# Seven products for eight in one dense layer, and an eigenvalue iteration moved ahead of it

## The chip, the cores and the metric

The kernel runs on one core of a Trainium2 chip. The metric is the device time of one execution in microseconds (us); lower is better. Three runs of the kernel before gave 2445.72, 2446.64 and 2447.99 us, a median of 2446.64.

The engines are named as in the profile: PE is the matrix engine TensorE (PEld its weight loads), DVE is VectorE, ACT is ScalarE, POOL is GpSimd, and SP is the queue that issues most DMA transfers. The built program is one list of instructions for each engine, and the trace shows every engine taking its own list in order; semaphores connect the lists.

## The reference, cut to what matters

Four layers follow each other on x of shape [128, 64, 256] (128 graphs of 64 nodes with 256 features), each with a residual connection and a layer norm. Everything is in fp32. The change lies in layer 0, and in the eigenvalue that layer 1 needs:

```python
# layer 0
A_norm = A + eye;  A_hat = A_norm * dinv[:, None] * dinv[None, :]
agg = einsum('nm,bmd->bnd', A_hat, features)
h   = relu(_batchnorm(agg @ W1.T + b1, g1, be1))      # 512 wide
out = _batchnorm(h @ W2.T + b2, g2, be2)              # 256 wide
x   = _layernorm(x + out)
# layer 1 begins with
lam_max = eigvalsh(L)[-1] + 1e-08
L_norm  = 2.0 * L / lam_max - eye
xp = einsum('mn,bnf->bmf', L_norm, x);  h = xp @ Wc + bc;  ...
```

Both batch norms take mean and variance over all 8192 rows. So no relu can start before the first dense product is complete for every row, and nothing after the second product can start before that one is complete for every row.

## The kernel before, in words

**Tiling.** The 8192 rows are cut into 16 blocks of 512 rows (`NBLK`, `TB`). A block's rows are spread over 128 partitions of two graphs each. Feature-major tiles hold 128 features on the partitions and the 512 rows along the free dimension; a helper `fm` views a buffer of 1024 columns as two such chunks. The two buffers of a block, `Xs[i]` and `H[i]`, hold the four chunks of the 512-wide hidden layer: chunks 0 and 1 in `Xs[i]`, 2 and 3 in `H[i]`.

**Layer 0.** `first_block(i)` loads a block (L525), multiplies it with `A_hat` on PE (`aggregate`, L320, eight matmuls of 128 columns), copies it out of PSUM on DVE (L535), multiplies it with W1 in two halves of four matmuls of 512 columns (`mm_fm`, L344), adds the bias on ACT (L547) and takes batch statistics on DVE (L551). When all 16 are done, `bn_coeffs` (L506 to L513) turns the statistics into a scale and a shift; the inverse root is one POOL instruction (L509). `second_block(i)` then applies relu with that scale and shift on ACT to the four chunks (L559), multiplies by W2 with eight matmuls of 512 columns (L564: two output chunks times four input chunks), adds the bias on ACT (L573), and takes statistics on DVE (L577). A second `bn_coeffs` follows, and `end_block` normalises (L636), transposes back on PE (L338), adds the residual (L644) and does the layer norm (L270, L272, L306, L309, L312).

**The eigenvalue.** `eig()` squares the 128 x 128 matrix M 26 times on PE (`EIG_STEPS`; L466). After each square, DVE takes the diagonal (L469, L471), PE sums it over the partitions with a matrix of ones (L474), and DVE takes the reciprocal of that trace (L477) and scales the square with it (L479). At the end L484 to L497 form the Rayleigh quotient and the matrix `LnT` that layer 1 multiplies with. `eig` has a PSUM buffer of its own (`e_ps`) out of four.

**Order.** The order of the work is made by a planner written in the kernel, `flow`. Tasks are generators that yield steps (engine, expected time, PSUM and SBUF buffers wanted); the planner always takes the step that can start soonest by its own estimate, with a margin of 2.0 us for PE steps, and of equal ones the task with the higher rank. In layer 0 there is one stream of at most six tasks at a time, and `eig` is the second task in it. The framework below may still move single instructions where their operands allow. The names that the text uses besides: `W2T` is W2 as loaded (L403), `Wc` to `W2` of layer 1 are loaded at L607 (W2 into the second half of `WB`), `end_block`'s input at L633, and at the head of the layers that follow L853 (wL), L370 (Wg, av), L860 (Wx), L379 (biases) and L896 (WT) are loads, L882 and L884 small products of the adjacency matrix with their copies L887 and L888, and L903 a product with one column (av).

Of the kernel before, what the change touches and what calls it, by code (L numbers as in the profile page):

```python
# [10 lines left out]
AF = mybir.ActivationFunctionType  # L11
# [4 lines left out]
P = 128  # L16
B, N, D = 128, 64, 256
NBLK = 16
TB = 512
# [14 lines left out]
def kernel(ctx: ExitStack, tc: tile.TileContext, a: dict, out: bass.AP):  # L34
# [15 lines left out]
    def fm(s):  # L50

        return s.rearrange("p (c k) -> p c k", c=2)
# [45 lines left out]
    class Stream:  # L98
# [3 lines left out]

        def __init__(self, width, prio, tasks):
            self.width, self.prio, self.tasks, self.n = width, prio, tasks, 0

    done = {}

# [3 lines left out]
    def ready(*keys):  # L113

        if all(k in done for k in keys):
            return max([0.0] + [done[k] for k in keys])
        return None

    def step(e, us, ps=0, sl=0, waits=True, at=None, tbl=None):

        return (e, us, ps, sl, waits, at, tbl)

    def flow(streams, margin):

        free = dict.fromkeys("TVSGQ", 0.0)
        table, running, now, seq = None, [], 0.0, 0
        while True:
            for s in streams:
                while s.tasks and s.n < s.width:
                    cond, body, peak = s.tasks[0]  # L140
                    t = 0.0 if cond is None else cond()
                    if t is None:
                        break
                    s.tasks.pop(0)
                    Clock.end, Clock.task = max(t, now), None
                    g = body()
                    if g is not None:
                        s.n += 1
                        seq += 1
                        running.append([(s.prio, seq), g, next(g), Clock.end, peak, 0, s])  # L150
                        running.sort(key=lambda r: r[0])
            if not running:
                assert not any(s.tasks for s in streams), "a task can't begin"
                return
            best, when, least = None, 0.0, 0.0
            lack = sorted((r[4] - r[5], r[5], r[0]) for r in running)

            def safe(r, sl):
                left = len(mem.free) - sl
                for short, held, rank in lack:  # L160
                    if r is not None and rank == r[0]:
                        short, held = short - sl, held + sl
                    if short > left:
                        return False
                    left += held
                return True

            mem.withdraw(lambda: safe(None, 1))
            for r in running:
                e, us, ps, sl, _, at, tbl = r[2]  # L170
                at = at() if callable(at) else at
                if r[2][5] is not None and at is None:
                    continue
                t = r[3] if at is None else at
                soon = max(t + margin.get(e, 0.0), free[e])
                t = max(t, free[e])
                if (ps <= 0 or len(PS.free) >= ps) and (sl <= 0 or (len(mem.free) >= sl and safe(r, sl))):
                    if ps > 0:
                        t = max(t, PS.free[0][0])
                        soon = max(soon, PS.free[0][0])  # L180
                    if sl > 0:
                        t = max(t, heapq.nsmallest(sl, mem.free)[-1][0])
# [27 lines left out]
    def ctile(shape, name, pool=cp):  # L210
        return pool.tile(shape, F32, tag=name, name=name)
# [152 lines left out]
    def by_chunk(ap):  # L364
        return ap.rearrange("(k p) m -> p k m", p=P)
# [19 lines left out]
    with c0:  # L385
# [7 lines left out]
        cols = {k: ctile([P, 4 if j < 3 else 2], f"l0{k}", wp) for j, k in enumerate(("b1", "g1", "be1", "b2", "g2", "be2"))}  # L393
        nc.scalar.dma_start(cols["b1"], a["L0_gnn_b1"])
        W2T = ctile([P, 4, D], "W2T", wp)

        def later_loads():
            for k in cols:
                if k != "b1":
                    yield step("Q", 1.0)  # L400
                    nc.sync.dma_start(cols[k], a[f"L0_gnn_{k}"])
            yield step("Q", 6.0)
            nc.sync.dma_start(W2T, by_chunk(a["L0_gnn_W2"]))  # L403
            yield step("V", 1.2)
# [36 lines left out]

        def eig():
            yield step("V", 1.2)
            V.tensor_scalar(Sy, Sy, 0.5, None, ALU.mult)
# [13 lines left out]
            V.tensor_scalar(sh, sh, 1e-30, None, ALU.add)  # L460
            M = etile("eM")
            V.scalar_tensor_tensor(M, ident, sh, Sy, ALU.mult, ALU.add)
            for _ in range(EIG_STEPS):
                yield step("T", 0.5)
                pm = pse(P)
                T.matmul(pm, M, M, start=True, stop=True)  # L466
                yield step("V", 0.6)
                t_ = etile("etmp")
                V.tensor_tensor(t_, pm, ident, ALU.mult)  # L469
                d_ = etile("ed", 2)  # L470
                V.reduce_sum(d_[:, 0:1], t_, axis=AX.X)  # L471
                yield step("T", 0.4)
                p_ = pse(2)
                T.matmul(p_[:, 0:1], ones, d_[:, 0:1], start=True, stop=True)  # L474
# [79 lines left out]
        def second_block(i):  # L554
            sc1, sh1 = bn["bn1"]
            src = [(fm(Xs[i]) if f < 2 else H[i])[:, f % 2, :] for f in range(4)]
            yield step("S", 2.8)
            for f in range(4):
                S.activation(src[f], src[f], AF.Relu, scale=sc1[:, f : f + 1], bias=sh1[:, f : f + 1])  # L559
            yield step("T", 6.9, ps=1)  # L560
            ps = PS.take()
            for c in range(2):
                for f in range(4):
                    T.matmul(  # L564
                        fm(PS[ps])[:, c, :],
                        W2T[:, f, c * P : (c + 1) * P],
                        src[f],
                        start=(f == 0),
                        stop=(f == 3),
                    )  # L570
            yield step("S", 1.3, ps=-1)
            for c in range(2):
                S.activation(H[i][:, c, :], fm(PS[ps])[:, c, :], AF.Identity, bias=cols["b2"][:, c : c + 1])  # L573
            PS.give(ps)
            yield step("V", 1.25)
            for c in range(2):
                V.bn_stats(st2[:, c, i, :], H[i][:, c, :])  # L577
            mark("l0b", i)

        blocks = range(NBLK)  # L580
        tasks = [(None, lambda i=i: first_block(i), 2) for i in blocks]
        tasks[1:1] = [(None, eig, 0)]
        tasks[4:4] = [(None, later_loads, 0)]
        tasks.append(
            (
                lambda: ready(*[("l0a", i) for i in blocks]),
# [1 line left out]
                0,  # L588
            )
        )  # L590
        tasks += [(lambda: ready(("bn1",)), lambda i=i: second_block(i), 0) for i in blocks]
        tasks.append(
            (
                lambda: ready(*[("l0b", i) for i in blocks]),
# [1027 lines left out]
```

## Time and profile before

| | |
|---|---|
| median of three runs | 2446.64 us |
| the profiled execution | 2449.05 us |
| its span, first to last instruction | 2447.3 us |
| PE busy in the span | 2362.6 us (97%) |
| DVE, ACT, POOL busy | 1208.8, 1152.1, 565.7 us |
| mean granted PE clock | 0.984 |
| first product's last W1 matmul starts a last time at | 155.2 us |
| second product L564, first start to last start | 161.7 to 277.0 us |
| first product of layer 1 (L320 with LnT) | 296.3 us |

Times within the kernel are microseconds from the start of the span of this one execution. An engine's busy time is the sum of its instructions; matmuls overlap in a pipeline and their ends are modelled, so the rate of a series of matmuls is read from the distance of their starts, not from the mean duration of one. In lists of groups, "x" is the number of instructions, then come busy time and mean duration in ns, and after the next bar how long the engine sat idle just before them and what it waited for.

### The profile page before, as it was taken

The page shows a single profiled execution, that of the slowest core. Times are in us where ns is not written, and L with a number is a line of the kernel's source. Part 1 is how long each engine was busy: PE and PEld are TensorE (multiplying, and loading weights), DVE is VectorE, ACT ScalarE, POOL GpSimd, SP SyncE. Part 2 cuts the span into 40 slices and gives each one's busy share as a digit, 9 for nine tenths or more (in the row PEclk, how much of TensorE's full clock was granted, in tenths as well). Part 3 has the DMA queues.
Part 4 walks back from the last instruction along what each step waited for, and adds up shares of the span by engine and source line. Part 5 has one row for each costly group of instructions (what it writes and reads, how often), then busy time and mean ns, then how long its engine had stood idle before and what let it go on. Part 6 is the DMA issues. An engine that isn't in the chain of part 4 may idle for free.

```text
span 2447.3 us, 33911 instructions
## 1 busy us (share of the span) xinstructions
PE 2362.6 (97%) x13700; PEld 1807.8 (74%) x13700; DVE 1208.8 (49%) x2868; ACT 1152.1 (47%) x2086; POOL 565.7 (23%) x426
## 2 busy tenths in 40 slices
PE   8999889989999999999999999999999999999986
PEld 5544566766775767666667888999999888888864
DVE  4542378564665455464442433354444554543465
ACT  2255454533444544444444444444435555653574
POOL 0000034231422233232322222222222222221111
PEclk9999899999999999999999999999999999999998
DMA  5110111100000000000010000000001001000201
GB/s 171 45 59 0 31 36 35 35 9 10 1 18 7 12 1 18 10 27 9 27 50 2 18 1 1 14 5 1 1 1 35 1 18 35 18 9 18 65 31 52
DMA packets 40973, 57.47 MB, mean 23 GB/s; under 512 B 4592, under 2 KB 33904, under 8 KB 40816
## 3 DMA queue, kind: packets, MB, share of 16 engines
q1 hardware_dynamic: 39712, 54.22, 6.8%
q8 instruction: 107, 1.75, 0.3%
q10 hardware_dynamic: 1104, 1.08, 0.1%
q14 instruction: 50, 0.41, 0.1%
HBM read 38.52 MB, written 16.78 MB: 23 GB/s over the span
## 4 chain that ended last, share of the span: by engine, by line
PE 73%; DVE 6%; ACT 4%; POOL 2%; issue 1%; POOLq 0%; ACTq 0%; DVEq 0%
PE ps L1022 24%; PE ps L950 13%; PE ps L344 10%; PE ps L356 5%; PE ps L833 4%; PE ps L320 3%; PE ps L703 2%; PE ps L1397 2%; PE ps L1159 2%; PE ps L1161 2%; DVE ln_st L270 1%; PE ps L332 1%; PE ps L776 1%; PE ps L1450 1%; ACT x L312 1%
## 5 line engine op out<-in xcount | busy, mean ns | idle before, releaser
L1022 PE MATMUL ps<-x,x 128*128 128x256 f32 x832 | 203.2, 379 | 0.7 <-DVE x L1090 0.7
L1022 PEld LDWEIGHTS ps<-x,x 128*128 128x128 f32 x832 | 155.0, 190 | 19.9 <-issue 1.1
L312 ACT ACTIVATE x<-x,ln_nm,ln_rs 128x256 f32<-128x256 f32 x176 | 92.9, 592 | 112.8 <-DVE ln_nm L309 112.8
L1022 PE MATMUL ps<-t,x 128*128 128x256 f32 x576 | 137.7, 380 | 0.0
L1022 PEld LDWEIGHTS ps<-t,x 128*128 128x128 f32 x576 | 108.4, 190 | 14.5 <-issue 0.4
L344 PE MATMUL ps<-t,W1T 128*128 128x512 f32 x256 | 115.1, 593 | 0.0
L306 POOL TENSOR_TENSOR ln_rs<-ln_rs,neghalf 128x4 f32<-128x4 f32 (+1 forms) x72 | 69.4, 964 | 189.7 <-DVE ln_rs L272 167.9
L950 PE MATMUL ps<-t,wL 128*128 128x512 f32 x216 | 94.5, 594 | 1.8 <-ACT t L1248 1.8
L292 POOL TENSOR_TENSOR ln_rs<-ln_rs,neghalf 128x4 f32<-128x4 f32 x32 | 35.9, 1122 | 239.5 <-DVE ln_rs L272 239.0
L950 PE MATMUL ps<-h,x 128*128 128x256 f32 x384 | 86.8, 379 | 0.0
L270 DVE BATCH_NORM_STATS2 ln_st<-x 128x6 f32<-128x256 f32 x224 | 85.5, 403 | 0.4
L962 ACT ACTIVATE t<-ps,bih 128x512 f32<-128x512 f32 (+3 forms) x108 | 63.5, 640 | 44.5 <-PE ps L950 44.4
L344 PE MATMUL ps<-t,wA 128*128 128x512 f32 x176 | 81.5, 608 | 2.6 <-ACT t L679 2.6
L1022 PE MATMUL ps<-h,x 128*128 128x256 f32 x320 | 82.5, 380 | 0.0
L1081 DVE COPY t<-ps 128x256 f32<-128x256 f32 (+2 forms) x58 | 21.6, 373 | 120.5 <-PE ps L1022 120.2
L344 PEld LDWEIGHTS ps<-t,W1T 128*128 128x128 f32 x256 | 46.3, 190 | 46.4 <-issue 46.4
L950 PEld LDWEIGHTS ps<-h,x 128*128 128x128 f32 x384 | 72.8, 190 | 10.2 <-issue 0.5
L950 PE MATMUL ps<-h,wL 128*128 128x192 f32 (+2 forms) x432 | 79.8, 338 | 0.0
L950 PEld LDWEIGHTS ps<-t,wL 128*128 128x128 f32 x216 | 40.7, 190 | 50.8 <-issue 47.1
L1098 ACT ACTIVATE x<-x,bih 128x512 f32<-128x512 f32 (+2 forms) x65 | 42.2, 650 | 76.2 <-DVE x L1088 73.9
L962 ACT ACTIVATE x<-ps,bih 128x512 f32<-128x512 f32 (+3 forms) x94 | 54.8, 636 | 45.6 <-PE ps L950 45.6
L950 PEld LDWEIGHTS ps<-h,wL 128*128 128x128 f32 x432 | 65.6, 190 | 11.4 <-issue 10.5
(681 smaller groups left out, 5765.3 us busy)
## 6 DMA issues: line engine op xcount, KB each, us to landing
t<-in_x_dram SPq DMA_DIRECT2D x28, 512.0 KB, 4.0
xd<-x SPq DMA_DIRECT2D x16, 512.0 KB, 2.6
x<-xd SPq DMA_DIRECT2D x5, 512.0 KB, 3.3
out_dram<-x SPq DMA_DIRECT2D x5, 512.0 KB, 2.9
wL<-in_L_gnn_Wih_dram SPq DMA_DIRECT2D x2, 1024.0 KB, 5.1
x<-in_L_gnn_Whh_dram SPq DMA_DIRECT2D x2, 1024.0 KB, 4.8
h<-in_x_dram SPq DMA_DIRECT2D x3, 512.0 KB, 5.0
t<-xd SPq DMA_DIRECT2D x3, 512.0 KB, 3.7
```

The costliest lines, as they stand in the source:

```text
L270: V.bn_stats(st[:, t, :], y[:, t, :])
L306: G.tensor_tensor(rs, rs, neghalf[:, :n], ALU.pow)
L312: S.activation(y[:, t, :], y[:, t, :], AF.Identity, scale=rs[:, t : t + 1], bias=nm[:, t : t + 1])
L320: T.matmul(ps[:, c, t * P : (t + 1) * P], y[:, t, c * P : (c + 1) * P], mT, start=True, stop=True,)
L344: T.matmul(ps[:, c, :], w[:, k, (off + c) * P : (off + c + 1) * P], yT[:, k, :], start=(k == 0), stop=(k == nk - 1),)
L356: T.matmul(ps[:, t, :], yT[:, k, t * P : (t + 1) * P], w[:, k, :], start=(k == 0), stop=(k == nk - 1),)
L703: T.matmul(pv[r * N : (r + 1) * N, b, :, :], x1T[:, k, b * N : (b + 1) * N], Wv_par[:, k, r, :, :], start=(k == 0), stop=(k == 1),)
L833: T.matmul(tm(PS[ps])[:, t, :], fm(mem[gs[k // 2]])[:, k % 2, t * P : (t + 1) * P], W2[:, k, :], start=(k == 0), stop=(k == 3),)
L950: T.matmul(spread(fm(PS[ps])[:, j, :n], q), WL[p][0][:, k, m], x_of(0, q)[:, k], start=(k == 0), stop=(k == 1),)
L962: S.activation(of(sl)[:, j], fm(PS[ps])[:, j, :n], AF.Tanh if g == 2 else AF.Sigmoid, bias=bias(g, c))
L1022: T.matmul(dst, WS[p][name](k, g), y[:, k], start=first and k == 0, stop=k == 1, skip_group_check=not first)
L1159: T.matmul(shaped(dst), WL[p][0][:, k, m], x[:, k], start=(k == 0), stop=False)
```

## The change

Three parts, all in layer 0.

The second product keeps its form for block 0 only, where it is now issued chunk by chunk: the relu of a chunk, then the two matmuls that use it. For blocks 1 to 15 the product is written with seven half-size products in place of eight (Strassen's form). The matrix W2 is cut in 2 x 2 quarters (each of 256 inputs and 128 outputs), and the block in input halves x, h and row halves u, v. DVE forms T1, T2 and T3 from differences of these quarters, POOL forms T4, and each of the seven products is two matmuls of 256 columns (L621 of the changed kernel). Partial results are taken out of PSUM on the way: two copies on ACT, one copy and two additions on DVE; the bias is added in three ACT instructions instead of two. Four combinations of quarters of W2 are formed once on DVE, and lie in the part of `WB` into which layer 1's W2 is loaded later.

In the eigenvalue iteration the trace is taken and divided out at every third square only; after the other squares DVE just copies the result out of PSUM.

`eig` becomes a stream of its own with the highest rank, whose steps have no margin in the planner, so that it runs as early as it can; the other tasks are the second stream. Its PSUM buffer is given back when it ends, and not after layer 0.

```diff
+        def __init__(self, width, prio, tasks, urgent=False):
...
-                soon = max(t + margin.get(e, 0.0), free[e])
+                soon = max(t if r[6].urgent else t + margin.get(e, 0.0), free[e])
...
+        W2S = WB[:, 2:4, :].rearrange("p a (b k m) -> p (a b) k m", b=2, k=2)
+        W2S = [W2S[:, j] for j in range(4)]
...
             nc.sync.dma_start(W2T, by_chunk(a["L0_gnn_W2"]))
+            yield step("V", 1.7)
+            (a11, a21), (a12, a22) = ([W2T[:, k : k + 2, c * P : (c + 1) * P] for c in range(2)] for k in (0, 2))
+            V.tensor_tensor(W2S[0], a21, a22, ALU.add)
+            V.tensor_tensor(W2S[1], W2S[0], a11, ALU.subtract)
+            V.tensor_tensor(W2S[2], a11, a21, ALU.subtract)
+            V.tensor_tensor(W2S[3], a12, W2S[1], ALU.subtract)
...
-            for _ in range(EIG_STEPS):
+            for j in range(EIG_STEPS):
                 yield step("T", 0.5)
                 pm = pse(P)
                 T.matmul(pm, M, M, start=True, stop=True)
+                if j % 3 < 2:
+                    yield step("V", 0.35)
+                    M = etile("eM")
+                    V.tensor_copy(M, pm)
+                    continue
...
             V.tensor_tensor(LnT, t_, ident, ALU.subtract)
+            PS.give(0)
...
         def second_block(i):
...
+            def relu(f):
+                S.activation(src[f], src[f], AF.Relu, scale=sc1[:, f : f + 1], bias=sh1[:, f : f + 1])
+            if i == 0:
+                for f in range(4):
+                    yield step("S", 0.7)
+                    relu(f)
+                    yield step("T", 1.75, ps=int(f == 0), waits=f == 3)
...
+                    for c in range(2):
+                        T.matmul(fm(PS[ps])[:, c, :], W2T[:, f, c * P : (c + 1) * P], src[f], start=(f == 0), stop=(f == 3))
...
+            x, h = fm(Xs[i]), H[i]
+            u, v = slice(0, TB // 2), slice(TB // 2, TB)
+            yield step("V", 1.4, sl=2)
...
+            V.tensor_tensor(T1, x[:, :, v], x[:, :, u], ALU.subtract)
+            V.tensor_tensor(T2, h[:, :, v], T1, ALU.subtract)
+            yield step("G", 1.3, waits=False)
+            G.tensor_tensor(T4, h[:, :, u], T2, ALU.subtract)
+            yield step("V", 0.7)
+            V.tensor_tensor(T3, h[:, :, v], x[:, :, v], ALU.subtract)
+            def product(w, y, dst, first=False):
+                for k in range(2):
+                    T.matmul(dst, w[:, k, :], y[:, k, :], start=first and k == 0, stop=k == 1, skip_group_check=not first)
...
+            p, y = (m.rearrange("p (j k) -> p j k", j=4) for m in (PS[ps], Xs[i]))
+            product(A11, x[:, :, u], p[:, 0, :], first=True)
+            product(W2S[0], T1, p[:, 3, :], first=True)
+            S.copy(y[:, 0, :], p[:, 0, :])
+            S.copy(y[:, 3, :], p[:, 3, :])
+            product(A12, h[:, :, u], p[:, 2, :])
+            product(W2S[3], h[:, :, v], p[:, 3, :])
+            product(W2S[1], T2, p[:, 0, :])
+            V.tensor_copy(y[:, 1, :], p[:, 0, :])
+            product(W2S[2], T3, p[:, 0, :])
+            V.tensor_tensor(y[:, 3, :], p[:, 0, :], y[:, 3, :], ALU.add)
+            V.tensor_tensor(y[:, 0:2, :], p[:, 2:4, :], y[:, 0:2, :], ALU.add)
+            product(A22, T4, p[:, 0, :])
+            S.activation(h[:, 0, :], fm(Xs[i])[:, 0, :], AF.Identity, bias=cols["b2"][:, 0:1])
+            S.activation(h[:, 1, v], y[:, 3, :], AF.Identity, bias=cols["b2"][:, 1:2])
+            S.activation(h[:, 1, u], p[:, 0, :], AF.Identity, bias=cols["b2"][:, 1:2])
...
-        tasks[1:1] = [(None, eig, 0)]
-        tasks[4:4] = [(None, later_loads, 0)]
+        tasks[3:3] = [(None, later_loads, 0)]
...
-        flow([Stream(6, 0, tasks)], {"T": 2.0})
-        PS.give(0)
+        flow([Stream(1, 0, [(None, eig, 0)], urgent=True), Stream(6, 1, tasks)], {"T": 2.0})
```

Between the seven products the generator yields a planner step for each, which the cut diff leaves out.

More of the change, by code (lines that the diff above doesn't have):

```diff
@@ L98 @@
     class Stream:
-        def __init__(self, width, prio, tasks):
+        def __init__(self, width, prio, tasks, urgent=False):
             self.width, self.prio, self.tasks, self.n = width, prio, tasks, 0
+            self.urgent = urgent
     done = {}
@@ L556, in second_block @@
             src = [(fm(Xs[i]) if f < 2 else H[i])[:, f % 2, :] for f in range(4)]
+            def relu(f):
[5 more added lines that the diff above has]
+                    yield step("T", 1.75, ps=int(f == 0), waits=f == 3)
+                    if f == 0:
+                        ps = PS.take()
+                    for c in range(2):
+                        T.matmul(
+                            fm(PS[ps])[:, c, :],
+                            W2T[:, f, c * P : (c + 1) * P],
+                            src[f],
+                            start=(f == 0),
+                            stop=(f == 3),
+                        )
+                yield step("S", 1.3, ps=-1)
+                for c in range(2):
+                    S.activation(H[i][:, c, :], fm(PS[ps])[:, c, :], AF.Identity, bias=cols["b2"][:, c : c + 1])
+                PS.give(ps)
+                yield from second_stats(i)
+                return
@@ L557, in second_block @@
             yield step("S", 2.8)
             for f in range(4):
-                S.activation(src[f], src[f], AF.Relu, scale=sc1[:, f : f + 1], bias=sh1[:, f : f + 1])
-            yield step("T", 6.9, ps=1)
-            ps = PS.take()
[L562 to L570, printed above, removed]
@@ L571, in second_block @@
-            yield step("S", 1.3, ps=-1)
-            for c in range(2):
-                S.activation(H[i][:, c, :], fm(PS[ps])[:, c, :], AF.Identity, bias=cols["b2"][:, c : c + 1])
+                relu(f)
+            x, h = fm(Xs[i]), H[i]
+            u, v = slice(0, TB // 2), slice(TB // 2, TB)
+            yield step("V", 1.4, sl=2)
+            slots = [mem.take() for _ in range(2)]
+            T1, T2, T3, T4 = (
+                mem[sl][:, j * TB : (j + 1) * TB].rearrange("p (c k) -> p c k", c=2) for sl in slots for j in range(2)
+            )
@@ new lines, in second_block @@
+            V.tensor_tensor(T1, x[:, :, v], x[:, :, u], ALU.subtract)
[6 more added lines that the diff above has]
+                for k in range(2):
+                    T.matmul(
+                        dst, w[:, k, :], y[:, k, :], start=first and k == 0, stop=k == 1, skip_group_check=not first
+                    )
@@ new lines, in second_block @@
+            A11, A12, A22 = (W2T[:, k : k + 2, c * P : (c + 1) * P] for k, c in ((0, 0), (2, 0), (2, 1)))
+            yield step("T", 1.75, ps=1)
+            ps = PS.take()
+            p, y = (m.rearrange("p (j k) -> p j k", j=4) for m in (PS[ps], Xs[i]))
+            product(A11, x[:, :, u], p[:, 0, :], first=True)
+            product(W2S[0], T1, p[:, 3, :], first=True)
+            yield step("S", 0.75, waits=False)
+            S.copy(y[:, 0, :], p[:, 0, :])
+            S.copy(y[:, 3, :], p[:, 3, :])
@@ new lines, in second_block @@
+            t = yield step("T", 1.75)
+            product(A12, h[:, :, u], p[:, 2, :])
+            product(W2S[3], h[:, :, v], p[:, 3, :])
+            yield step("T", 0.88)
+            product(W2S[1], T2, p[:, 0, :])
+            yield step("V", 0.42)
+            V.tensor_copy(y[:, 1, :], p[:, 0, :])
+            yield step("T", 0.88)
+            product(W2S[2], T3, p[:, 0, :])
+            yield step("V", 1.1)
+            V.tensor_tensor(y[:, 3, :], p[:, 0, :], y[:, 3, :], ALU.add)
+            V.tensor_tensor(y[:, 0:2, :], p[:, 2:4, :], y[:, 0:2, :], ALU.add)
@@ L574, in second_block @@
+            yield step("T", 0.88)
+            product(A22, T4, p[:, 0, :])
+            for sl in slots:
+                mem.give(sl)
+            yield step("S", 1.5, ps=-1)
+            S.activation(h[:, 0, :], fm(Xs[i])[:, 0, :], AF.Identity, bias=cols["b2"][:, 0:1])
+            S.activation(h[:, 1, v], y[:, 3, :], AF.Identity, bias=cols["b2"][:, 1:2])
+            S.activation(h[:, 1, u], p[:, 0, :], AF.Identity, bias=cols["b2"][:, 1:2])
             PS.give(ps)
+            yield from second_stats(i)
@@ L575, in second_block, with second_stats @@
+        def second_stats(i):
             yield step("V", 1.25)
@@ L590 @@
         )
-        tasks += [(lambda: ready(("bn1",)), lambda i=i: second_block(i), 0) for i in blocks]
+        tasks += [(lambda: ready(("bn1",)), lambda i=i: second_block(i), 2) for i in blocks]
         tasks.append(
```

## The prediction

> **What bounds the kernel now.** First the page's slices: how busy TensorE (PE) is, and which clock it was granted.
>
> ```profile
> PE   8999889989999999999999999999999999999986
> ...
> PEclk9999899999999999999999999999999999999998
> ```
>
> PE is at 9 tenths or more nearly everywhere, so a shorter PE stage ends earlier unless another engine fills the gap. The change lies in slices 1 to 5 (0 to 300 us). The table by stretches (PE, PEld, DVE, ACT, POOL busy, then clock) shows where PE has slack:
>
> ```profile
> core 0: us, PE busy (x) PEld busy (x) DVE busy (x) ACT busy (x) POOL busy (x), PEclk, DMA share, GB/s
> 140.00:160.00 20.00, 17.09 (x60) 9.14 (x58) 12.15 (x27) 5.76 (x10) 0.92 (x1) 0.99 0.33 105
> 160.00:180.00 20.00, 18.76 (x45) 9.04 (x45) 4.90 (x16) 19.22 (x29) 0.10 (x1) 0.84 0.01 1
> 240.00:260.00 20.00, 20.00 (x53) 9.24 (x52) 5.43 (x12) 3.80 (x6) 0.00 (x0) 1.00 0.00 0
> 280.00:300.00 20.00, 11.57 (x54) 10.77 (x55) 10.90 (x45) 13.59 (x22) 3.18 (x7) 0.57 0.30 94
> ```
>
> At 240:260, inside the second product, PE is full, DVE at 5.4 and ACT at 3.8 of 20 us: PE alone sets the time. At 160:180 the clock averages 0.84 (the product starts on a cold array); at 280:300 PE is busy 11.6 of 20: the hand-over to layer 1 is a chain, not a load. The chain of waits gives rates from runs without a gap:
>
> ```profile
> 781.94 10.30 PE ps L344 x24
> ...
> 1515.72 22.45 PE ps L1022 x104
> ```
>
> Every fp32 matmul shows as two records. 512 columns: 10.30/24 x 2 = **0.858 us**; 256 columns: 22.45/104 x 2 = **0.432 us**, so halving the columns halves the time. The timeline prices an eigenvalue round:
>
> ```profile
> 130.13 0.38 PE L466 MATMUL ps<-eM 128*128 128x128 f32 x2
> ...
> 130.35 3.60 PE L344 MATMUL ps<-t,W1T 128*128 128x512 f32 x8
> ...
> 133.78 0.28 PE L474 MATMUL ps<-ed,ones 128*128 128x1 f32 x2
> ...
> 133.93 2.03 PE L320 MATMUL ps<-AhT,t 128*128 128x128 f32 x16
> ```
>
> A square (L466) holds PE from 130.13 to 130.35, 0.22 us; a trace (L474) from 133.78 to 133.93, 0.15 us. The second product runs from 161.71 to E = 277.48: 115.8 us = 128 x 0.858 (109.8) + some 11 rounds x 0.37 (4.1) + 1.9 of cold clock and waits. Then comes the chain into layer 1:
>
> ```profile
> 281.77 0.29 DVE L484 TENSOR_TENSOR etmp<-eM,Sy 128x128 f32<-128x128 f32 x1
> ...
> 282.95 8.57 ACT L636 ACTIVATE h<-h,bn2sh,bn2sc 128x512 f32<-128x512 f32 x12 [3.94 <-DVE bn2sh L513]
> ...
> 285.66 1.94 PE L338 MATMUL ps<-ident,h 128*128 128x128 f32 x8 [2.38 <-DVE rb L888]
> ...
> 292.90 3.54 PE L903 MATMUL ps<-av,t 128*128 128x1 f32 x16 [1.95 <-DMA av<-in_L_gnn_a_dram]
> ...
> 296.30 2.05 PE L320 MATMUL ps<-LnT,x 128*128 128x128 f32 x8
> ```
>
> DVE's eigenvalue tail (L484 to L497, until 284.7) and two copies behind it hold the first transpose L338 until 285.66, E+8.2; layer 1's first products (L320) start at E+18.8, the second block's end at E+24.1. Last, what the new instructions cost, by equal shapes elsewhere in this kernel (layer 2 has the same seven-product form), and a collision:
>
> ```profile
> L1060 ACT COPY x<-ps 128x256 f32<-128x256 f32 x34 | 12.4, 366 | 21.5 <-PE ps L1022 21.5
> ...
> L1081 DVE COPY x<-ps 128x256 f32<-128x256 f32 x34 | 14.3, 422 | 59.6 <-PE ps L1022 59.5
> ...
> L1126 DVE TENSOR_TENSOR x<-x,t 128x1024 f32<-128x1024 f32 x7 | 8.6, 1222 | 0.4
> ...
> L1042 POOL TENSOR_TENSOR x<-h 128x512 f32<-128x512 f32 x7 | 9.4, 1338 | 41.1 <-DVE h L1284 23.2 <-PE ps L1022 10.2 <-DVE x L997 7.6
> ```
>
> ```profile
> 1818.84 2.35 POOL L1115 TENSOR_TENSOR t<-x,t 128x1024 f32<-128x1024 f32 x1 [14.16 <-ACT t L1102]
> ...
> 1819.45 2.56 DVE L1123 TENSOR_TENSOR t<-t,x 128x768 f32<-128x768 f32 x1 [1.43 <-ACT x L1102]
> ```
>
> [...] weight loads take 0.34 instead of 0.19 us from 162.7 to 166.4, after PE's idle 157 to 161. [...] L1123 took 2.56 us beside L1115 (768 elements took 0.96 at L1138). [...]
>
> **The change, part by part** (placements are read from the order in which the built programs put instructions on each engine; from layer 1's start on the two orders are all but the same).
>
> 1. Products. 15 blocks go from 8 x 0.858 = 6.87 to 14 x 0.432 = 6.04 us: **-12.3**. Beside PE a block now needs: ACT 4 relus at 0.71 (two L559 step by 1.41), copies 0.37 + 0.38, outputs 0.72 + 0.50 + 0.47: 5.3 us; DVE three subtractions 2.07, copy 0.42, adds 0.42 + 0.69, statistics 1.37: 5.0, or 4.4 as neighbours overlap by 0.08; POOL 1.34. All are below 6.04, so PE stays the bound on average. Hidden by PE; without that cover ACT would be next.
>
> 2. Eigenvalue rounds. 18 of 26 traces go, and everything moves ahead of the second product: there **-4.1**. The first product holds 26 squares and 8 round traces instead of 15 and 15: 11 x 0.22 - 7 x 0.15 = **+1.4**, and at the start, where PE is cold, the first square and trace cost double: **+0.4**. Squares are spaced by 1.9 to 3.4 us of other PE work and wait only for a 0.35 us copy: no further stall.
>
> 3. W2 combinations. Four DVE adds stand right after the first aggregate's copy. DVE is in order; behind them are the second aggregate's copy, then the copy that the third square waits for, and behind that square stands all of PE. W2T landed at 11.06 + 3.8 = 14.9; its load now has one x block more ahead and is issued about 0.4 later: 15.3. Then two adds (0.4 each), copy 1.22, copy 0.35: the square starts near 17.8 instead of 16.5: **+1.3**. If W2T lands at 14.9 it is +0.9, at 18.0 it is +3.9.
>
> 4. Before the second product the trace has 5.1 us (155.64 to 160.78) of bn1 work; eigenvalue work slips out of DVE: **-0.1**. PE starts cold as before; block 0's chunks let it start at the first relu, as it does today, but its second chunk is the sixth relu: cold clock and waits 2.6 against 1.9, **+0.7**.
>
> 5. Waits inside the product. Of a block's five groups the last three each wait for an ACT or DVE hand-over, but two to four other groups (0.86 each) stand between. ACT runs ahead on relus: before block 5's copies it has 39 relus (27.5 us), five pairs of copies (3.3), block 0's output (1.3) and most of three others (4.1), done 36.4 us after the first relu; PE is there at 0.9 + block 0's 6.9 + 29 groups (25.0) + 2.6 = 35.4. So block 5 waits 1.1, and block 6 by the same count 0.55: **+1.7**. From there ACT has 43 us of work against PE's 66. At the end no other block is left: the last one waits for its copy and for statistics that stand ahead of its add on DVE (1.3 together), and the three adjacency products (L882, L884; idle-time work today) move inside with 0.87, less what they fill: **+2.1**. Waits that I didn't find, mostly collisions of POOL's subtraction with DVE's 45: the trace can't show them here; 0 to 4, taken **+0.8**.
>
> 6. Into layer 1. Without the eigenvalue tail the transpose starts at E+5.9 instead of E+8.2: -2.2. But SP's W2 load of layer 1 goes into the buffer of the combinations and waits for the last product; behind it are one x block, wL, Wg, Wx, av, biases and WT (loaded early today). And the 3.5 us of L903, which today run while PE waits for the normalised block, stand after layer 1's first matmul; a third residual add precedes the normalisation on DVE (1.2). Laid out: relus from E+4.7, first transposed block E+7.9, its residual add 9.2, normalised 16.2 to 17.7, L903's work 17.0 to 20.5, first block's products done 22.5; the second block's scale stands on DVE behind the copy of L903's result (20.9), its products end at E+24.4 against E+24.1 today. The 2.2 are spent: **+0.3** net (between -2.2 and +2).
>
> Sum: -12.3 - 4.1 + 1.4 + 0.4 + 1.3 - 0.1 + 0.7 + 1.7 + 2.1 + 0.8 + 0.3 = **-7.8 us**. The profiled execution took 2449.05 (span 2447.3 and 1.75 around it), 0.1% above the median 2446.64; there 2441.2, as a median **2438.8**. With the bounds of 3, 5 and 6 this case covers about 2434 to 2446. A measurement tells about 0.2%, 4.9 us, from no change.
>
> **Rivals.**
> - A: the hand-over saves what it frees (L903's place costs nothing): -10.3, 2436. For it: E+8.2 is DVE's doing. Against: the new order.
> - B: in-order queues eat it. W2T late (+3.9 instead of 1.3) and the ACT waits doubled: -7.8 + 2.6 + 1.7 = -3.5, 2443, no difference that can be told. For it: ACT is full at 160:180 already.
> - C: [...] If two of three DVE subtractions per block wait for POOL's whole 1.34, DVE needs 4.4 + 2.7 = 7.1 per block and becomes the bound: 15 x (7.1 - 6.04) = +15.9 instead of 0.8, in all +7.3, 2454. It decides from 6.86 us per block on, where all of 0.82 is gone. For it: L1123's 2.56. Against: layer 2's products of this form show PE gaps of under 1 us, POOL works 1.3 of 6 us.
> - D: the change does something else. The built order has 210 matmuls of 256 columns and 8 of 512: excluded.
>
> **Numbers.** Forecast 0.56, A 0.10 (faster 0.66), B 0.21, C 0.13. Range 2433 to 2448: A's and B's values are in, C is not.
>
> **What would show it.** The second product takes 104 to 106 us from first to last matmul, PE full in its middle; PE's first W1 product near 18 us; the last one of the first phase near 158.7; E near 269; layer 1's first product 19 to 21 us after E. Wrong if PE shows gaps in mid-product, if a DVE subtraction averages over 1.2 us, or if the first phase grows by over 5 us.

## The result and the profile after

The changed kernel took 2444.03 us, the median of 20 runs (2438.57 to 2447.93), against 2446.89 us for the kernel before in 20 runs beside them (2445.40 to 2449.49). The ratio is 0.9984, with a 95% interval of 0.9977 to 0.9990: about 4 us faster (the medians differ by 2.9), but less than the 0.2% that the prediction called a clear difference. A second series of 21 runs gave 0.9984 again (0.9978 to 0.9991). The forecast was 7.8 us less. The profiled execution took 2443.38 us with a span of 2441.6.

The slices of the page after, PE and its clock. PE's row is digit for digit that of before; the clock has an 8 in the fifth and the sixth slice (244 to 366 us), before in the fifth alone, so PE was at half clock (0.50 in the trace's clock record) for longer there, 34.1 us of these two slices against 23.9 before:

```profile
PE   8999889989999999999999999999999999999986
...
PEclk9999889999999999999999999999999999999998
```

The table by stretches after (PE, PEld, DVE, ACT, POOL busy, then clock):

```profile
160.00:180.00 20.00, 15.83 (x46) 9.43 (x47) 10.27 (x20) 16.70 (x27) 6.91 (x5) 0.83 0.01 1
240.00:260.00 20.00, 20.00 (x94) 17.40 (x93) 11.70 (x22) 7.72 (x17) 3.19 (x3) 1.00 0.20 54
280.00:300.00 20.00, 18.13 (x93) 16.63 (x93) 8.04 (x22) 14.49 (x23) 2.02 (x2) 0.70 0.18 49
```

In the middle of the second product PE is still full (20.00 of 20) while DVE does 11.7 and ACT 7.7: the matmuls still bound it. The stages stand in PE's timeline after:

```profile
17.61 0.49 PE L478 MATMUL ps<-eM 128*128 128x128 f32 x2 [1.44 <-DVE eM L482]
17.94 2.31 PE L346 MATMUL ps<-t,W1T 128*128 128x512 f32 x5
...
152.60 5.74 PE L346 MATMUL ps<-t,W1T 128*128 128x512 f32 x13
164.17 6.29 PE L587 MATMUL ps<-x,W2T 128*128 128x512 f32 x8 [5.83 <-ACT x L577]
...
267.50 1.10 PE L621 MATMUL ps<-t,W2T 128*128 128x256 f32 x4 [1.22 <-DVE x L645]
...
283.81 0.80 PE L322 MATMUL ps<-LnT,x 128*128 128x128 f32 x2 [0.47 <-ACT x L314]
284.40 0.63 PE L340 MATMUL ps<-ident,h 128*128 128x128 f32 x2
284.82 3.41 PE L984 MATMUL ps<-av,t 128*128 128x1 f32 x16
288.10 5.54 PE L322 MATMUL ps<-LnT,x 128*128 128x128 f32 x30
293.47 3.62 PE L358 MATMUL ps<-wA,t 128*128 128x256 f32 x16
...
333.54 8.62 PE L346 MATMUL ps<-t,wA 128*128 128x512 f32 x16 [7.48 <-ACT t L760]
```

The second product runs from 164.17 to 268.60 (267.50 + 1.10, a modelled end), 104.4 us; by the same measure it took 115.9 us before (161.71 to 277.64). The first matmul with Wc (L358) starts at 293.47; its twin in the kernel before (L356) at 301.42. So the changed kernel **leads by 7.95 us** there, almost exactly the forecast sum. Then the lead goes. The same matmul, the first of block 1's product with Wq, stands in the kernel before at:

```profile
338.46 7.13 PE L344 MATMUL ps<-t,wA 128*128 128x512 f32 x16 [2.57 <-ACT t L679]
```

Here PE waited 2.57 us for ACT's copy, after the change 7.48: the lead is 4.92. The eight products behind it take 8.62 instead of 7.13 us, as they start while the clock is at half (0.50 from 329.7 to 336.5 us by the trace's clock record). At 388.75 us of the kernel before (first product with W1) the lead is 2.07, at 549.00 us 0.66.

The wait is a chain over three engines, seen in the timelines of POOL, DVE and ACT after (each from its own view):

```profile
329.11 2.34 POOL L798 TENSOR_TENSOR t<-t,rows 128x1024 f32<-128x1024 f32 x1
```

```profile
329.17 2.29 DVE L311 SCALAR_TENSOR_TENSOR ln_nm<-ln_mv,ln_rs 128x4 f32<-128x4 f32 x1 [0.86 <-POOL ln_rs L308]
```

```profile
331.50 1.09 ACT L314 ACTIVATE x<-x,ln_nm,ln_rs 128x256 f32<-128x256 f32 x2 [3.92 <-DVE ln_nm L311]
332.50 0.99 ACT L760 COPY t<-ps 128x1024 f32<-128x1024 f32 x1
```

L311 has four elements per partition and a median of 0.16 us over its 72 instances. Here it starts 0.06 us after POOL's addition of bo (L798) and takes 2.29 us, POOL's whole instruction. ACT's L314 waits for it, and behind L314 in ACT's list stands L760, for which PE waits. In the kernel before this layer-norm group (of a block that layer 1 needs much later) stood behind block 1's copy on ACT, and behind the first steps of the first softmax on DVE (L745, L746).

### The profile page after: what moved, and what is told of

Its sections match the earlier page's. It is cut to its first block, busy times and chain, and to the rows that moved or that the text cites. A ratio compares the mean times of both kernels' runs of the same rounds, so it can differ in the third digit from the quotient of the medians.

```text
span 2441.6 us, 34351 instructions
## 1 busy us (share of the span) xinstructions
PE 2348.3 (96%) x13844; PEld 1837.1 (75%) x13844; DVE 1255.2 (51%) x2908; ACT 1164.8 (48%) x2131; POOL 585.0 (24%) x441
## 4 chain that ended last, share of the span: by engine, by line
PE 76%; DVE 8%; issue 7%; ACT 6%; POOL 1%; DMA 0%; ACTq 0%; POOLq 0%; DVEq 0%
PE ps L1103 24%; PE ps L1031 13%; PE ps L346 11%; PE ps L358 5%; PE ps L914 4%; PE ps L322 3%; PE ps L784 2%; PE ps L621 2%; PE ps L1478 2%; DVE ln_st L272 2%; PE ps L1240 2%; PE ps L1242 2%; PE ps L334 1%; PE ps L857 1%; PE ps L1531 1%
## 5 line engine op out<-in xcount | busy, mean ns | idle before, releaser
L314 ACT ACTIVATE x<-x,ln_nm,ln_rs 128x256 f32<-128x256 f32 x176 | 93.0, 592 | 113.0 <-DVE ln_nm L311 113.0
L346 PE MATMUL ps<-t,W1T 128*128 128x512 f32 x256 | 114.7, 594 | 0.0
L346 PE MATMUL ps<-t,wA 128*128 128x512 f32 x176 | 82.1, 611 | 7.5 <-ACT t L760 7.5
L346 PEld LDWEIGHTS ps<-t,W1T 128*128 128x128 f32 x256 | 46.6, 190 | 48.3 <-issue 48.3
L1179 ACT ACTIVATE t<-t,bih 128x512 f32<-128x512 f32 (+2 forms) x58 | 37.1, 642 | 77.9 <-DVE t L1169 77.8
```

Of the source, the lines that this page charges most:

```text
L314: S.activation(y[:, t, :], y[:, t, :], AF.Identity, scale=rs[:, t : t + 1], bias=nm[:, t : t + 1])
L346: T.matmul(ps[:, c, :], w[:, k, (off + c) * P : (off + c + 1) * P], yT[:, k, :], start=(k == 0), stop=(k == nk - 1),)
L1179: S.activation(of(act[g])[:, 0], of(act[g])[:, 0], f, bias=bias(g, 0))
```

## The experiments

All leads below are times on PE: when the kernel before's profiled execution starts a matmul, less when the kernel in question does. The points are 301.42 us (first product with Wc), 338.46 (Wq, block 1), 388.75 (W1) and 549.00 us of the kernel before; "end" compares the spans. There is one profile of the kernel before, so whatever was chance in it stands in every lead. A ratio compares a kernel with the runs of the kernel before in its own series, so kernels of different series are compared by their ratios rather than by their medians.

| kernel | runs | median us | ratio, 95% interval | lead at 301 | at 338 | at 389 | at 549 | end |
|---|---|---|---|---|---|---|---|---|
| changed | 20 | 2444.03 | 0.9984 (0.9977 to 0.9990) | 7.95 | 4.92 | 2.07 | 0.66 | 5.7 |
| changed, again (e1) | 21 | 2441.50 | 0.9984 (0.9978 to 0.9991) | 7.60 | 4.59 | 2.55 | 2.48 | 7.7 |
| planned as before (e2) | 5 | 2433.57 | 0.9956 (0.9943 to 0.9968) | 12.57 | 12.61 | 12.61 | 12.36 | 15.5 |
| the same, again (e10) | 5 | 2433.54 | 0.9948 (0.9935 to 0.9960) | 11.08 | 11.12 | 10.15 | 10.04 | 13.3 |
| seven products only (e3) | 13 | 2445.51 | 0.9994 (0.9986 to 1.0003) | 5.50 | 2.05 | -0.44 | -0.61 | 4.5 |
| e3 planned as before (e8) | 10 | 2441.17 | 0.9973 (0.9964 to 0.9983) | 10.05 | 9.68 | 9.68 | 9.75 | 10.1 |
| eigenvalue only (e4) | 13 | 2446.71 | 1.0001 (0.9993 to 1.0009) | 2.92 | 2.91 | 1.59 | 1.66 | 1.7 |
| no bo in block 1 (e5) | 18 | 2442.66 | 0.9984 (0.9977 to 0.9991) | 7.53 | 6.65 | 3.76 | 3.53 | 6.6 |
| e2, W2 sums on POOL (e6) | 5 | 2431.51 | 0.9938 (0.9924 to 0.9951) | 13.42 | 13.44 | 13.41 | 13.04 | 17.9 |
| e2, T4 on DVE (e7) | 5 | 2432.82 | 0.9944 (0.9931 to 0.9956) | 12.47 | 12.45 | 11.44 | 11.27 | 16.2 |
| e2, both (e9) | 5 | 2435.25 | 0.9948 (0.9935 to 0.9962) | 14.52 | 14.50 | 14.48 | 14.25 | 17.3 |

The last column has a part that no edit made. Between 549 us and the end the lead grows by 0.1 to 5.2 us, though nothing was changed there. The kernel before's profiled execution lost time there, and at 2449.05 us it lies above every median of that kernel (2445.99 to 2448.45 in the series of this study). Two of its stretches by the table (the clock is the third number from the right), and the same of the changed kernel:

```profile
1200.00:1225.00 25.00, 22.07 (x141) 16.64 (x140) 18.49 (x56) 6.70 (x10) 8.84 (x6) 0.86 0.06 22
2400.00:2415.00 15.00, 13.41 (x66) 7.67 (x63) 7.94 (x34) 10.07 (x25) 2.01 (x2) 0.77 0.21 71
```

```profile
1200.00:1225.00 25.00, 22.07 (x147) 17.06 (x146) 18.97 (x57) 6.70 (x10) 8.85 (x6) 0.93 0.05 22
2400.00:2415.00 15.00, 12.41 (x76) 8.07 (x76) 9.31 (x45) 9.81 (x26) 3.64 (x4) 1.00 0.11 36
```

Clock 0.86 and 0.77 against 0.93 and 1.00: the kernel before spent more time at half clock there. So a lead is read at 549 us, and a total is judged by the series of runs.

**e1, the changed kernel again**, without an edit.

> The changed kernel once more, for a second profile and for runs beside the other kernels of this call. Theory 1 (the order made from layer 1 on costs it): the lead over the kernel before, read at the first products of layer 1 with LnT, is 8.0 to 8.8 us again, and 4 to 5 us of it go again between there and 340 us, with an L311 on DVE of over 2 us beside POOL's L798 and a wait of PE of over 6 us for ACT L760. Theory 2 (chance: stretches of half clock fall differently in each run): the lead at layer 1 is the same, but L311 takes 0.16 us and the loss lies elsewhere or is absent. Total by both: 2 to 5 us below the kernel before.

L311 took 2.29 us again, PE waited 7.0 us for L760, and the lead fell from 7.60 to 2.48. The collision belongs to the order; it is no accident of one run. The second theory holds in part: for what lies behind 549 us, and for some of the loss between 341 and 549 us. The first profile has half clock (0.50) from 370.7 to 377.5 us, which cost it 2.7 us of lead between 376.02 and 380.83 us of the kernel before; e1 has it for 3.4 us there, which cost 1.3.

**e2, planned as before.** The planner's second call, for layers 1 to 3, starts from the times at which it believes the buffers free. Only these bookkeeping times are replaced:

```diff
+    for q, ts in ((PS, (265.59, 272.99, 280.29, 285.82)),
+                  (mem, (116.5, 122.65, 126.1, 132.25, 135.7, 141.85, 145.3, 153.1))):
+        q.free = [(t, j) for t, (_, j) in zip(ts, sorted(q.free))]
     flow(
         lends
```

From layer 1's first matmul on, the order is then that of the kernel before on every engine, but for two transposes on PE, two L717 on ACT and the copy L993 on DVE; layer 0 is the changed kernel's.

> The changed kernel, but the planner starts layer 1 with the free times of PSUM and SBUF buffers that it had in the kernel before, so that all engines have the order of the kernel before from layer 1 on; layer 0 is untouched. Theory 1 (the new order in layer 1 costs 4 to 5 us): 7 to 9 us below the kernel before, 3 to 5 below the changed kernel; in the trace the lead at the first products with LnT is 7 to 9 us and is still over 6 us at the L346 that answers to 338.46 us of the kernel before. Theory 2 (chance): total within 1.5 us of the changed kernel.

2433.57 us, and in a second series (e10) 2433.54: more than theory 1 asked for. The lead is 12.57 us at the first Wc product and 12.36 at 549 us; almost nothing is lost in layer 1. At 301 us the lead is already 4.6 us larger than the changed kernel's; 0.5 of this was there at the end of the second product, so the new order cost some 4 us in the hand-over as well. PE's timeline of e2:

```profile
279.87 3.54 PE L984 MATMUL ps<-av,t 128*128 128x1 f32 x16 [1.36 <-DMA av<-in_L_gnn_a_dram]
283.27 5.73 PE L322 MATMUL ps<-LnT,x 128*128 128x128 f32 x32
288.84 3.62 PE L358 MATMUL ps<-wA,t 128*128 128x256 f32 x16
...
325.85 7.13 PE L346 MATMUL ps<-t,wA 128*128 128x512 f32 x16 [2.26 <-ACT t L760]
```

L984 now runs while PE has nothing else; in the changed kernel it stands between the first and the second matmul of the LnT product and puts 3.3 us (284.82 to 288.10) in front of the rest. The wait for L760 is 2.26 us instead of 7.48: on ACT, L760 starts at 324.81, right behind the layer-norm group before, and the group that held it stands behind it.

> The kernel planned as before from layer 1 on a second time, for a second profile and runs beside the kernel with all three edits. Lead at the first products with Wc 12 to 13 us again, total 2433 to 2437; if its first result was a lucky draw of half-clock stretches, the total lies above 2437.

The total, 2433.54 us, is in the range. The lead at 301 us is 11.08, not 12 to 13: the second product took 104.35 us between first and last start (103.54 in e2), and the hand-over 0.7 us more. Another 1.3 us went at a half-clock stretch from 364.5 to 367.9 us, so the old order loses lead to such stretches too.

**e3, seven products only.** The eigenvalue iteration as before:

```diff
-            for j in range(EIG_STEPS):        # trace at every third square
+            for _ in range(EIG_STEPS):        # trace at every square
...
-        flow([Stream(1, 0, [(None, eig, 0)], urgent=True), Stream(6, 1, tasks)], {"T": 2.0})
+        flow([Stream(6, 0, tasks)], {"T": 2.0})   # eig is the second task
```

> Seven products as in the changed kernel, but the eigenvalue iteration as in the kernel before: second task of the one stream, trace at every square. By the steps of the prediction the second product takes 115.8 - 12.3 + 5.3 = 108.8 us from first to last matmul, the first phase is up to 1.3 us longer than before, and the eigenvalue tail holds the hand-over as before: lead at layer 1 some 5 us. Theory 1: the order from layer 1 on is that of the changed kernel, so 4 to 5 us go there and the total is within 2 us of the kernel before. Theory 2: total 4 to 6 us below.

The product took 107.5 us between first and last start. The lead of 5.50 us was gone by 389 us, and the total can't be told from the kernel before's, as theory 1 had it. The first phase was 4.9 us longer, not 1.3, as PE waited 2.9 us for the first copies behind the W2 combinations and then worked at half clock from 17 to 24 us (the first four matmuls of L346 took 6.77 us); in e8, whose layer 0 is the same, the wait was 1.5 us and no such stretch followed (3.70 us).

**e8, e3 with e2's edit.**

> Seven products with the eigenvalue iteration of the kernel before, and planned as in the kernel before from layer 1 on. Theory 1 (the new order from layer 1 on costs each kernel that has it 6 to 8 us): the lead at the end of the second product is 3 us as with the seven products alone (2.96 us), the hand-over keeps the eigenvalue tail and is as in the kernel before, so total 3 us below the kernel before, about 2443, and 2.5 to 3 below the seven products alone; with the kernel planned as before this leaves the eigenvalue part 9 us. Rival (the order matters only where eigenvalue work is out of the way): total within 1 us of the seven products alone, 2445.5.

2441.17 us, 4.3 below e3 (by the ratios, 0.9973 against 0.9994, about 5), and 9.75 us of lead kept at 549 us. From 301 to 549 us e8 loses 0.3 us of lead, e3 6.1. So the order costs the seven products alone as well; how much of it shows in the totals isn't settled, as e3's profile also lost time in the first phase. The lead at the end of the product was 6.4 us, not 3 (last start 270.62 against 277.05), as e3's loss in the first phase was absent; it grew to 10.05 in the hand-over, since DVE had finished the eigenvalue tail before the product ended. The tail was expected to stay; with seven products it was out of the way in e8 with the old form of the iteration too.

**e4, eigenvalue only.** Eight products as before, no W2 combinations, the new iteration in its own stream. As in the changed kernel, the tasks of the second product have rank 2 in the planner instead of 0, a line that the diff further up leaves out.

> Eight products as in the kernel before, but the eigenvalue iteration as in the changed kernel: own urgent stream, trace at every third square. By the steps of the prediction the first phase is 1.4 + 0.4 us longer, the second product 4.1 us shorter, and the hand-over 2.2 us shorter as the eigenvalue tail is off DVE: lead at layer 1 4.5 us. The order from layer 1 on is that of the kernel before. Theory 1: it keeps the lead, total 3.5 to 5 us below the kernel before, so as fast as the changed kernel. Theory 2: the total may be anything between 0 and 6 below.

The lead is 2.92 us at 301 us, and 1.66 at 549; the total doesn't differ from the kernel before (interval 0.9993 to 1.0009). Theory 1 said 3.5 to 5, so it fails here: this kernel has the old order and still keeps little. Of the 4.5 us forecast at layer 1 only 2.9 arrived: the first phase was 2.1 us longer (forecast 1.8), the product 3.7 shorter (4.1), the hand-over 1.3 shorter (2.2). Its half-clock stretches after 300 us add up to 62.3 us, those of the kernel before to 55.5. Whether that is the draw or a property of its waits was not settled. On top of the seven products the medians give the new iteration 7.6 us (2441.17 in e8, 2433.57 in e2), the leads at 549 us only 2.6 (e2) or 0.3 (e10); how much of it is its own stays open too.

**e5, no bo in block 1.**

```diff
-        yield step("G", 2.4, waits=False)
-        G.tensor_tensor(y, y, row["bo"], ALU.add)
+        if i != 1:
+            yield step("G", 2.4, waits=False)
+            G.tensor_tensor(y, y, row["bo"], ALU.add)
```

> The changed kernel without one instruction: POOL's addition of the bias bo to block 1 in layer 1 (the second L798), so that block's attention output lacks this bias. The order on all other engines stays. Theory 1 (the collision of this instruction with L311 on DVE holds ACT's L314, behind it ACT's L760 and so PE): L311 at 329 us takes 0.16 us instead of 2.29, PE's wait for ACT L760 falls from 7.0 or 7.5 us to about 5, and the lead at the L346 behind it grows by 1.8 to 2.2 us against the changed kernel; total about 2 us below it, 2439. Rival (ACT or DVE have other work that ends as late): L311 is short, but L346 starts within 0.5 us of its old place.

DVE's and PE's timelines of e5:

```profile
329.58 0.16 DVE L311 SCALAR_TENSOR_TENSOR ln_nm<-ln_mv,ln_rs 128x4 f32<-128x4 f32 x1 [0.86 <-POOL ln_rs L308]
```

```profile
331.82 9.76 PE L346 MATMUL ps<-t,wA 128*128 128x512 f32 x16 [5.27 <-ACT t L760]
```

L311 is back at 0.16 us, PE's wait at 5.27, and the lead at 338 us is 6.65 instead of 4.59 to 4.92. The collision costs 1.7 to 2.1 us at its place, as expected. In the total it can't be told: 2442.66 us instead of the 2439 expected, and the ratio is that of the changed kernel. Part of the gain went at once, as the eight products behind L760 started earlier within the stretch at half clock and took 9.76 us instead of 8.62 (9.14 in e1); the lead at 389 us is 3.76, against 2.07 and 2.55. The other 2.7 us of the wait (5.27 against 2.57 before) come with the layer-norm group that stands ahead of block 1's copy on ACT. e2 puts it back together with the rest of the old order; no run moves this group alone.

**e6, W2 combinations on POOL**, on top of e2: `V.tensor_tensor(W2S...)` becomes `G.tensor_tensor(W2S...)`, four times.

> The kernel planned as before from layer 1 on, with one more edit: the four combinations of quarters of W2 are formed on POOL, which is idle then, instead of DVE. The order of all other instructions stays. By step 3 of the prediction the third square loses its wait for the copy behind the first two additions (1.44 us in the trace): first W1 product at 16.4 to 16.7 us instead of 17.9, and the gain of 1.3 to 1.5 us is still there at layer 1; total 1.3 to 1.5 us below the kernel planned as before, about 2432. Rival (the second block's data or its copy come as late anyway): first W1 product later than 17.4 us, total unchanged.

PE's timeline of e6:

```profile
16.83 0.39 PE L478 MATMUL ps<-eM 128*128 128x128 f32 x2
17.05 2.31 PE L346 MATMUL ps<-t,W1T 128*128 128x512 f32 x5
```

The wait of 1.44 us is gone, but the first W1 product moves by 0.9 us, not 1.4: the third aggregate, ahead of it, started at 15.04 us in this execution and at 14.22 in the changed kernel's. In e2, on which e6 builds, it started at 15.16 and the wait was 0.55 us. The lead at 301 us grows by 0.85 against e2. At 2431.51 us this is the lowest median of the study, but the interval of its ratio overlaps that of e2, so a gain in the total isn't shown.

**e7, T4 on DVE**, on top of e2: `G.tensor_tensor(T4...)` becomes `V.tensor_tensor(T4...)`.

> The kernel planned as before from layer 1 on, with T4 formed on DVE instead of POOL[...]; DVE gets 15 x 0.69 us more, 5.1 to 5.7 us of 6.04 per block. If the exclusion of DVE and POOL costs time in the product (rival C of the prediction, and the reserve of 0.8 in step 5), the second product, 103.5 to 104.1 us between first and last start, gets shorter by 0.5 to 1 us and the total with it. If PE hides it all, the product stays within 0.3 us, and DVE's overlong subtractions (up to 1.69 us, mean 0.75) go back to 0.69 with nothing gained; it may get longer by up to 1 us if DVE's load begins to show at the end of the product.

The view of the line of T2 (L613; minimum, median and maximum in ns), first the changed kernel, then e7:

```profile
L613 DVE TENSOR_TENSOR t<-h,t x15: 670/681/1686, 167.0 to 243.2; 128x512 f32<-128x512 f32 x15
```

```profile
L613 DVE TENSOR_TENSOR t<-h,t x15: 675/685/694, 166.9 to 242.1; 128x512 f32<-128x512 f32 x15
```

With POOL out of the product no subtraction of this line is held: 0.69 us at most, against 1.69. The product takes 102.9 us between first and last start, against 103.5 to 104.4 in the six executions that have the new iteration and T4 on POOL. So what POOL held up cost 0.7 to 1.5 us, far from deciding; in e7 the lead at 301 us is 12.47, no more than in e2, so the hand-over took it back.

**e9, e6 and e7 together.**

> Three edits together: planned as before from layer 1 on, the combinations of quarters of W2 on POOL, T4 on DVE. If they are independent: first W1 product near 17.0 us, second product 102.9 us between first and last start, lead at layer 1's first products with Wc 0.9 + 0 to 0.7 us more than planned as before alone; total 2430.5 to 2431.5. If the shorter product is taken back in the hand-over, as with T4 on DVE alone (lead at layer 1 unchanged), the total is that of the W2 combinations on POOL, 2431.5.

The lead is the largest, 14.25 us at 549 us, but the median of five runs is 2435.25 us (2431.26 to 2435.93), not the 2430.5 to 2431.5 expected, with a ratio of 0.9948: no gain over e2 or e6 that these runs can tell.

## Why the prediction was right where it was, and where it failed

- **Products, waits and tail inside the second product (steps 1, 2 and 5):** forecast -12.3 - 4.1 + 0.7 + 1.7 + 2.1 + 0.8 = -11.1 us; measured 104.43 - 115.93 = -11.5. Right as a sum. The product started at half clock again (0.50 from 162.5 to 169.3 us; before from 159.4 to 166.3). The 0.69 us of a subtraction on DVE, of which step 1's 2.07 is made, was the author's estimate; L612, L613 and L617 have medians of 0.693, 0.681 and 0.683. The ACT waits of blocks 5 and 6 were overpriced: PE's waits for L633 add up to 0.5 us, not 1.7 (and the terms listed for ACT in step 5 add up to 36.2 us, not 36.4, so block 5's wait comes to 0.8 by that count); at the end PE waited the 1.2 us for the last addition (L645).
- **First phase (steps 2 and 3):** forecast +1.4 + 0.4 + 1.3 = +3.1; the last W1 product starts at 157.75 instead of 155.21, +2.5. The first trace (L465) held PE from 7.73 to 8.15 us and the first square (L478) from 11.70 to 12.13, 0.42 and 0.43 us where a trace took 0.15 and a square 0.22 at 130 to 134 us in the kernel before: the doubling that step 2 prices at 0.4. The third square started at 17.61 (forecast 17.8) behind the additions on DVE; e6 showed that they cost 0.9 us.
- **Into layer 1 (step 6):** forecast -2.2 + 2.5 = +0.3 from the product's end. From there to the first Wc product it took 23.8 us before (277.64 to 301.42), 24.9 after, +1.1. Both terms were larger: with the old order (e2) it is 20.7 us, so 3.1 were freed and 4.2 spent. The place of L984 was named and its price right (3.3 us): one matmul with LnT starts 15.2 us after the product's end, the other fifteen 19.5 us after it. The W2 load of layer 1, blamed there too, isn't what the last loads waited for: in e2 it is issued at 265.61, the x block behind it at 268.16, and wL only at 271.88.
- **The step that failed** is the parenthesis at the head of the parts, "from layer 1's start on the two orders are all but the same", and so a sum without a term for layer 1. At 301.42 us the lead was 7.95 us, the forecast's -7.8; that it fits so well is partly luck, as the first phase cost 0.6 us less than forecast, the product gained 0.4 more, and the hand-over cost 0.8 more. The orders do agree for most of their length, but not on DVE and ACT in the first 55 us of layer 1, where every block is a chain from engine to engine. One layer-norm group ahead of block 1's copy, with the collision, cost 3.0 us up to 338 us in both profiles. Behind it the lead fell by another 4.3 us by 549 us (2.1 in e1): 1.5 us at the eight products at half clock (2.0 in e1) and 2.7 at the later stretch of half clock (1.3 in e1), with small gains and losses between. With the old order (e2) the loss is gone but for 0.2 us (1.0 in e10, which has such a stretch); which single displaced instruction costs how much was measured for L798 alone.
- **Rival B** has the fitting number, 2443 us, but not the mechanism: the in-order queues did eat half of the gain (PE's 7.48 us of waiting for L760, which stands behind L314 in ACT's list), yet in layer 1 and not by a late W2T or by ACT in the product.
- **Rival C** had DVE wait for a whole instruction of POOL, and looked for it in the wrong place. The runs show such a wait: 2.29 us for L311 beside L798's 2.34, 0.16 without L798 (e5). In the product these waits cost 0.7 to 1.5 us, in layer 1 one instruction of four elements cost 2. Why DVE waits was not shown.
- **Rival A** (the hand-over saves what it frees, -10.3 us, 2436) is what the old order gives, and somewhat more: 2433.57 us in e2, 12.4 below the kernel before in its series.
- **Range and chances:** 2444.03 lies in 2433 to 2448, by the width of the range and not because the sum was complete. 0.66 on a clear gain was too much: the interval of the ratio, 0.9977 to 0.9990, lies mostly within 0.2%.

## What to carry to other kernels

When an edit shortens one stage of a kernel whose order a planner makes, compare the orders behind that stage on every engine, above all at the head of the next one, where blocks are still chains and any engine's list can be on the critical path; a longest common ending says nothing on the part that matters. Follow the lead matmul by matmul instead of comparing totals: it shows in one table which stage made a gain and which took it back. A planner's state at a stage's border is part of the change: putting back the order that had been good for the next stage was worth more here (2433.5 against 2441.5 to 2444.0 us) than the whole change had brought.

## What the runs showed of the hardware that was not expected

- A four-element instruction on DVE held for 2.29 us by POOL's 1024-element addition (e5: 0.16 without). Its size did not tell what it could lose.
- Stretches at half clock (0.50 in the clock record) were between 3.4 and 20.5 us long, about multiples of 3.4, and added up to 47 to 62 us after 300 us in each profile. They fell in different places in executions of the same program: at 519 to 522 us in e1 but not in the first profile of the changed kernel, where the clock was 1.00 there (and at 17 to 24 us in e3 but not in e8, whose layer 0 is the same). What starts them was not shown. The price of a gap of PE varied by run: behind the same idle of PE, 2.75 to 2.84 us long and ended by DVE between 363 and 376 us, there was half clock for 6.8 us in the first profile of the changed kernel, for 3.4 in e1 and e10, and none in the kernel before and e2. The changed kernel's 20 runs spread over 9.4 us, against 4.1 of the kernel before; that these stretches are the reason is not shown.
